# Block sums of an attention turned over by VectorE instead of TensorE, and layer 0's loads, flag and last nodes in another order

## The chip, the core and the metric

The kernel runs on one core of one Trainium2 chip, in one launch. The metric is device time in microseconds. A core has five engines that run side by side, each with its own queue of instructions in program order: TensorE (PE, matmul; its weight loads are listed as PEld), VectorE (DVE), ScalarE (ACT), GpSimd (POOL) and SyncE (SP, which here only issues DMAs). They meet through semaphores. SBUF is the working memory, PSUM the memory that matmuls write.

## The reference

There are N = 3327 nodes with D = 128 features and an adjacency matrix of 0 and 1. Layer 0 is a graph convolution, layer 1 an attention.

```python
# layer 0
h = max(layernorm(x), 0)
deg = adj.sum(1);  deg = where(deg == 0, 1, deg)
t = (adj.T @ h / deg) @ W_n.T + b_n + h @ W_c.T + b_c
x = x + relu(gamma * batchnorm(t) + beta)
# layer 1
h = max(layernorm(x), 0)
q, k, v = ((h @ W.T).reshape(128, 3327, 8) for W in (Wq, Wk, Wv))
a = softmax(q @ k.T / sqrt(128) + adj + adj, axis=2)     # 128 batches of 3327 x 3327
out = x + (a @ v).reshape(3327, 1024) @ Wo.T
```

The reshape doesn't split heads: it cuts the flat product into 128 batches of 3327 rows of 8 numbers.

## The kernel before

**Layer 0.** Nodes are cut into NC = 26 chunks of 128. For each chunk c a tile `a` of adj (128 x 3327) is loaded by SP (L431), PE adds `A[:, c, :].T @ a` into seven PSUM banks `acc` (L433), ScalarE sums the rows into `deg` (L437), VectorE takes their largest entry `amax` (L440), and one small piece of other work runs beside it (`beside`: turning the normalised nodes A into B, the product with W_c, the norms of Wq and Wk with GpSimd squares L406; `spread`: the reciprocals of deg laid along the columns, L410). x and the weights are loaded by DMAs issued from ScalarE's queue, x in two parts of 8 and 17 chunks, ahead of ScalarE's first work; all chunks are normalised (`stats`, `normalise`; L359 is VectorE's mean times reciprocal) before the loop over chunks.

Behind the loop, for each of the seven blocks of 512 columns: the mean (L506), the product with W_n (L507), the sum and its statistics (`hidden`); in between `spread` for the last two groups of chunks, and `set_flag` (L477), which computes from amax and the norms whether the softmax can go without a shift. Then batch norm and relu, residual, second layer norm, the columns of h in B, the projections of the first group of batches (`project_now`), the loads of its k, q and v, and writes to DRAM: `xd` (the nodes), `hd` (the columns of h), `wd` (exp(2 adj) for the last 8 chunks, a part of it; the rest is made during the first group).

**Attention.** The 128 batches are taken in NG = 32 groups of G = 4. The 3328 columns (queries) are cut into 7 blocks of QB = 476, the last 472. For each group and block, 26 chunks of 128 keys are gone through in SU = 13 steps, so there are 224 blocks and 2912 steps. A step takes four pairs (chunk, half); a half is two of the four batches. For each pair PE makes scores `s` for two batches side by side (`product`, L750), into one of three PSUM buffers of two banks each, which go round. Pairs are of two kinds:

- plain: VectorE adds adj to the scores (`add`, L862, which reads the tile `at` from SBUF and s from PSUM and writes a part of `d`); all plain pairs of a step then go through one exponential of ScalarE (L907), which is issued one step late.
- weighted: ScalarE takes the exponential f straight from s (L871) and GpSimd multiplies it by the loaded exp(2 adj), `wt` (L874).

Steps 3, 7 and 11 (`DOUBLE`) have two plain and two weighted pairs, all others three plain and one weighted. In a step the order is: the product and exponential of the first weighted pair; the exponential L907 of the step before; product and add of the first plain pair; half of the weighted sums of three steps earlier (`second(0)`, L623, PE); product and add of the second plain pair; the fourth pair; the other half of the sums (`second(1)`). In the step after a double one (4, 8, 12) the first product of the next step stands ahead of `second(1)`. Data for two steps later are requested by SP at a step's start (`fetch(x + PRE)`).

The sums of a block pile up in one of two PSUM tiles `av`: for batch b, rows 32b to 32b + 7 are the 8 sums and row 32b + 8 is the softmax denominator, all over the block's columns. They are finished by `finish`, a generator that goes on by one `yield` in each of the steps that `PARTS` names, in the block that follows (a block's last sums are issued in step 2 of the next one). Before: VectorE copies av into avs in step 3 (L633); PE turns it over by matmuls with a part of the identity in steps 5 and 6 (L640, two matmuls of the program in each, which the profile shows as four); in step 7, where `step()` stands between the first and the second add, VectorE takes the maximum of the denominators with 1e-30 (L648), the reciprocal (L649) and the product (L651); in step 8 SP stores the result to `att` (L658).

Later projections and the output product (`projections`, `outputs`: L208, L214, L234, L236, L269, L271, L279, L284) are slipped in at the end of steps 7 and 11, one part at a time, through the av tile that isn't in use. k of the next group is loaded into `ks` and sorted by GpSimd casts (L192).

The order on each engine is the program's: the kernel turns the framework's scheduler off (`manual_schedule`).

Of the kernel before, what the change touches and what calls it, by code (L numbers as in the profile page):

```python
# [20 lines left out]
H = 8  # L21
# [5 lines left out]
QB = 476  # L27
# [9 lines left out]
PARTS = (3, 5, 6, 7, 8)  # L37
# [9 lines left out]
def tile_two_layer_gnn(  # L47
# [42 lines left out]
    xd = dram.tile([NP, D], F32, name="xd")  # L90
# [13 lines left out]
    nc.gpsimd.memset(ov, 1.0)  # L104
    zeros = const.tile([P, H], F32, name="zeros")
# [98 lines left out]
    def projection(wk, hj, j, s, e, quick, ov, factor):  # L204
# [8 lines left out]
        if s == 2:  # L213
            nc.vector.tensor_copy(  # L214
                ov[:CH, e * 64 : (e + 1) * 64, :H],
                bank[:CH].rearrange("p (u h) -> p u h", h=H),
            )
            yield
            if e:
                nc.sync.dma_start(  # L220
                    v1[tok, :].rearrange("(p u) h -> p u h", u=D), ov[:CH]
                )
            return
        o = wk.tile([P, 2, NB], F32R, name="o")
        factor = 1.0 if s else factor
        if quick:
            nc.scalar.activation(o[:CH, 0], bank[:CH], AF.Copy, scale=factor)
            nc.vector.scalar_tensor_tensor(
                o[:CH, 1], bank[:CH], factor, o[:CH, 0].bitcast(F32), ALU.mult, ALU.subtract
            )  # L230
        else:
# [3 lines left out]
            else:  # L235
# [3 lines left out]
                o[:CH, 1], f[:CH], o[:CH, 0].bitcast(F32), ALU.subtract  # L239
            )  # L240
        yield
        for a in range(2):
            g = a * H + e * (H // 2)
            nc.sync.dma_start(
                (qT, kT)[s][g : g + H // 2, tok].rearrange("g (p u) -> p g u", u=D),
                o[:CH, a].bitcast(F32).rearrange("p (h u) -> p h u", u=D),
            )

    def projections(wk, hj, j, quick, ov, factor):
        return [  # L250
            projection(wk, hj, j, s, e, quick, ov, factor) for s in (1, 0, 2) for e in range(2)
        ]

    def outputs(wk, j):
# [7 lines left out]
        nc.sync.dma_start(xj[:CH], xd[j * CH : (j + 1) * CH, :])  # L262
# [38 lines left out]
    with tc.tile_pool(name="l0", bufs=1) as l0, tc.tile_pool(  # L301
        name="l0adj", bufs=3
    ) as ap, tc.tile_pool(name="l0s", bufs=2) as sp, tc.tile_pool(
# [18 lines left out]

        xr = x[: (NC - 1) * P, :].rearrange("(c p) d -> p c d", p=P)
        nc.vector.memset(xs[:, NC - 1, :], 0.0)
        for c0, c1 in ((0, 8), (8, NC - 1)):
            nc.scalar.dma_start(xs[:, c0:c1, :], xr[:, c0:c1, :])
        for p0, p1 in pieces(N - (NC - 1) * P):
            nc.scalar.dma_start(
                xs[p0:p1, NC - 1, :], x[(NC - 1) * P + p0 : (NC - 1) * P + p1, :]
            )  # L330
        nc.scalar.dma_start(wc, WcT)
        for i, b in enumerate((b_n, b_c, gamma, beta)):
            nc.scalar.dma_start(cols[:, i : i + 1], b.rearrange("o d -> d o"))
        nc.scalar.dma_start(wn, WnT)
        for t, w in zip(wqk, (WqT, WkT, WvT)):
            nc.scalar.dma_start(t, w)
        nc.scalar.dma_start(wo, WoT.rearrange("(e p) o -> p e o", p=P))
# [43 lines left out]
        stats(0)  # L381
        for i in range(NQ):
            if i + 1 < NQ:
                stats(i + 1)
            normalise(i, A)
        nc.vector.tensor_add(bias, cols[:, 0:1], cols[:, 1:2])

        def beside(x):
# [4 lines left out]
            elif x < 2 * NQ:  # L393
                n0 = (x - NQ) * NB
# [7 lines left out]
            elif x < 2 * NQ + 4:  # L402
                i = x - 2 * NQ
                sq = sp.tile([P, NB], F32, name="sq")
# [5 lines left out]
        def spread(i):  # L410
# [7 lines left out]
            dg = sp.tile([P, 4, P], F32, name="dg")  # L418
            for j in range(n):
                nc.gpsimd.tensor_scalar(  # L420
                    dg[:, j, :], ident, rdeg[:, 4 * i + j : 4 * i + j + 1], None, ALU.mult
                )
            nc.tensor.matmul(
# [4 lines left out]

        for c in range(NC):
            a = ap.tile([P, 7 * NB], F32, name="a")  # L430
            nc.sync.dma_start(a[:, :N], adj[c * P : (c + 1) * P, :])  # L431
            for i, (n0, w) in enumerate(blocks):
                nc.tensor.matmul(  # L433
                    acc[i][:, :w], A[:, c, :], a[:, n0 : n0 + w],
                    start=(c == 0), stop=(c == NC - 1),
                )
            nc.scalar.activation(  # L437
                junk, a[:, :N], AF.Copy, accum_out=deg[:, c : c + 1]
            )
            nc.vector.tensor_reduce(  # L440
                amax[:, c : c + 1], a[:, :N], AX.X, ALU.max, apply_absolute_value=True
            )
            if c >= 1:
                beside(c - 1)

            i = c - 2 * NQ - 5
            if 0 <= i < NQ - 2 and 4 * i + 4 <= c:
                spread(i)
        weights = []
        for n0 in range(0, NB, NB // 2):  # L450
            a = ap.tile([P, 7 * NB], F32, name="a")
            a8 = a[:, : 8 * (NB // 2)].rearrange("p (c n) -> p c n", c=8)
            nc.sync.dma_start(a8, adjr[:, WC:, n0 : n0 + NB // 2])
            weights.append((a8, n0, NB // 2))

        def weigh_early():
            a8, n0, w = weights.pop(0)
            nc.scalar.activation(a8, a8, AF.Exp, bias=low, scale=2.0)
            nc.sync.dma_start(wd[:, :, n0 : n0 + w].rearrange("c p n -> p c n"), a8)
# [5 lines left out]
        nc.vector.tensor_reduce(top, amax, AX.X, ALU.max)  # L465
        b = l0.tile([1, 6], F32, name="bound")
        for i in range(2):
            nc.vector.tensor_tensor(
                b[:, i : i + 1], norm[:, 2 * i : 2 * i + 1], norm[:, 2 * i + 1 : 2 * i + 2],
                ALU.max,  # L470
            )
        nc.vector.tensor_tensor(b[:, 0:1], b[:, 0:1], b[:, 1:2], ALU.mult)
        nc.vector.tensor_scalar(
            b[:, 0:1], b[:, 0:1], (1.001 * D * H * HALF) ** 2, None, ALU.mult
        )

        def set_flag():  # L477
# [9 lines left out]
            nc.vector.tensor_scalar(b[:, 5:6], b[:, 2:3], HALF, None, ALU.mult)  # L487
            nc.tensor.matmul(aside[:, :2], ones[:1, :P], b[:, 4:6], start=True, stop=True)
            nc.vector.tensor_copy(low_half, aside[:, :2])

# [13 lines left out]
        for i, (n0, w) in enumerate(blocks):  # L504
# [5 lines left out]
            if i in (0, 2):  # L510
                spread(NQ - 2 + i // 2)
            if i == 3:
                set_flag()
            if i in (4, 6):
                weigh_early()
# [16 lines left out]
        def keep_nodes(cs):  # L532
            nc.sync.dma_start(
                xd.rearrange("(c p) d -> p c d", p=P)[:, cs, :], xs[:, cs, :]
            )

        def residual(i):
            pt, cs = turned(i, A, acc[i])
            nc.vector.tensor_add(xs[:, cs, :], xs[:, cs, :], pt)
            if i < 3:  # L540
                keep_nodes(cs)

        def second_norm(i, engine):

            for c in range(4 * i, min(NC, 4 * i + 4)):
                engine.tensor_scalar(
                    C[:, c, :], xs[:, c, :], rs[:, c : c + 1], mr[:, c : c + 1],
                    ALU.mult, ALU.add,
                )
# [8 lines left out]
        def keep_columns(i0, i1):  # L558
            s = slice(4 * i0 * P, min(NC, 4 * i1) * P)
            nc.gpsimd.dma_start(hd[:, s], B2[:, s])  # L560

        def project_now(j, banks):
            todo = projections(sp, B2[:, j * CH : (j + 1) * CH], j, True, ov, low_half[:CH, 1:2])
            for p, b in zip(todo, banks):
                drive(p, b)
            for p in todo:
                drive(p)
                drive(p)
# [12 lines left out]
        stats(1, False)  # L581
        residual(2)
        project_now(0, [acc[j] for j in (6, 5, 4, 0)] + [aside, acc[1]])

        q, k, v = sets[0]
        ks = sets[1][1].rearrange("p c n -> p (c n)")
        for b in range(G):
            for args in k_loads(ks, 32 * b, b, 0, NP):
                nc.sync.dma_start(*args)
        for args in v_loads(v, 0):  # L590
            nc.sync.dma_start(*args)
        for i in range(4, NQ):
            relu(i)

        for b in range(G):
            for args in q_loads(q, 32 * b, b, 0, NB):
                nc.scalar.dma_start(*args)
        for i in range(2, NQ):
            if i > 2:
                residual(i)  # L600
            stats(i, False)
        nc.gpsimd.dma_start(
            xd.rearrange("(c p) d -> p c d", p=P)[:, 12:, :], xs[:, 12:, :]
        )
        roots(4, NC)
        factors(4, NC)
        for i in range(1, NQ):
            second_norm(i, nc.gpsimd if i % 3 == 0 else nc.vector)
        for i in range(1, NQ):
            columns(i, i % 2 == 0)  # L610
        for x, c in enumerate(range(0, NC, 4)):
            n = min(4, NC - c)
            (nc.scalar.copy if x % 2 else nc.gpsimd.tensor_copy)(
                k[:, c : c + n, :],
                ks.bitcast(F32).rearrange("g (p c) -> g c p", c=NC)[:, c : c + n, :],
            )
        keep_columns(0, NQ)
# [499 lines left out]
```

## Time and profile before

| | |
|---|---|
| time, median of 3 runs | 10375.15 us (10374.6 to 10377.76) |
| the profiled execution's own time | 10381.98 us |
| its span, first to last instruction | 10380.2 us |
| PE, ACT, DVE, POOL busy | 96%, 96%, 90%, 81% of the span |
| first step of the attention | about 264 us from the start |
| mean granted TensorE clock | 0.992 |

An engine's busy time is the time that its instructions cover; a matmul's end is modelled, so a busy PE is not PE at its peak. In the groups of instructions a row gives line, engine, operation, what is written and read, shapes and count, then busy time in us and the mean of one in ns, and then the idle time of the engine just before these instructions with what ended most of it. In a row of a window the columns are the window, its length, busy time (and instructions) of PE, PEld, DVE, ACT and POOL, then the granted clock, DMA share and GB/s. In a timeline row the columns are start, length (of several equal instructions together where a count stands behind), engine, line and operation; idle time ahead of it stands in brackets.

### The profile page before, as it was taken

How to read it: one execution, taken by the hardware profiler on the slowest of the kernel's cores; microseconds unless marked ns; L12 is line 12 of the kernel's file. 1: busy time of each engine (PE TensorE's matmuls, PEld its weight loads, DVE VectorE, ACT ScalarE, POOL GpSimd, SP SyncE). 2: the span in 40 equal slices, each digit the busy share in tenths (PEclk: the TensorE clock that was granted, in tenths of full speed). 3: DMA queues.
4: the chain of work that ended last, by engine and by line, in shares of the span. 5: the costliest groups of instructions: out<-in, count | busy, mean ns of one | idle time of the engine just before them, and what ended most of it. 6: DMA issues, size and time to landing. Idle time of an engine off the chain costs nothing. (4 is left out here: it accounts for less than half of the span.)

```text
span 10380.2 us, 189900 instructions
## 1 busy us (share of the span) xinstructions
PE 9995.3 (96%) x73327; PEld 3082.3 (30%) x73327; DVE 9366.9 (90%) x9533; ACT 9923.2 (96%) x6655; POOL 8439.0 (81%) x4317
## 2 busy tenths in 40 slices
PE   7899999999999999999999999999999999999999
PEld 3222222222222222222222222222222222222222
DVE  5789999999999999999999999999999999999998
ACT  4899999999999999999999999999999999999998
POOL 1678888888888888888888888888888888888887
PEclk9899999999999999999999999999999999999999
DMA  6766666666666666666665666666666665666554
GB/s 228 221 177 164 163 170 167 166 165 165 163 166 170 165 165 162 164 168 167 167 164 159 168 167 168 167 161 162 167 169 167 167 161 159 171 169 167 157 153 127
DMA packets 1114449, 1735.99 MB, mean 167 GB/s; under 512 B 194622, under 2 KB 1089980, under 8 KB 1105852
## 3 DMA queue, kind: packets, MB, share of 16 engines
q1 hardware_dynamic: 1108766, 1716.94, 60.9%
q8 instruction: 575, 9.42, 0.4%
q10 hardware_dynamic: 4350, 4.20, 0.1%
q14 instruction: 342, 2.80, 0.1%
q0 software_dynamic: 416, 2.63, 0.1%
HBM read 1621.05 MB, written 102.38 MB: 166 GB/s over the span
## 5 line engine op out<-in xcount | busy, mean ns | idle before, releaser
L862 DVE SCALAR_TENSOR_TENSOR d<-at,s 128x952 f32<-128x952 f32 x8064 | 8797.4, 1141 | 681.7 <-PE s L750 397.6
L874 POOL TENSOR_TENSOR f<-f,wt 128x952 f32<-128x952 f32 (+1 forms) x3584 | 7939.0, 2233 | 1674.3 <-ACT f L871 1649.9
L907 ACT ACTIVATE d<-d 128x2856 f32<-128x2856 f32 (+1 forms) x2912 | 7027.9, 2413 | 2.2 <-DVE d L862 1.9
L623 PE MATMUL av<-d,v 128*9 128x476 f32 x32256 | 5065.6, 566 | 0.7 <-ACT d L907 0.7
L750 PE MATMUL s<-q,k 32*128 32x476 f32 x23296 | 4087.3, 475 | 313.8 <-ACT f L871 243.5
L871 ACT ACTIVATE f<-s 128x952 f32<-128x952 f32 (+1 forms) x3584 | 3396.9, 970 | 281.8 <-PE s L750 266.0
L750 PEld LDWEIGHTS s<-q,k 32*128 32x128 f32 x23296 | 1739.5, 182 | 5500.2 <-DVE d L862 3005.9
L623 PE MATMUL av<-f,v 128*9 128x476 f32 x14336 | 2849.0, 566 | 0.0
L623 PEld LDWEIGHTS av<-d,v 128*9 128x9 f32 x32256 | 583.3, 88 | 1161.5 <-issue 1149.6
L640 PE MATMUL av<-ident,avs 128*119 128x36 f32 (+1 forms) x1792 | 474.1, 391 | 0.8 <-DVE avs L633 0.8
L640 PEld LDWEIGHTS av<-ident,avs 128*119 128x119 f32 (+1 forms) x1792 | 422.9, 308 | 103.1 <-issue 101.5
L623 PEld LDWEIGHTS av<-f,v 128*9 128x9 f32 x14336 | 316.6, 88 | 112.4 <-issue 88.7
L192 POOL CAST k<-ks 128x256 fp32r<-128x256 f32 x434 | 283.8, 654 | 0.0
L433 PE MATMUL acc<-a,A 128*128 128x512 f32 (+1 forms) x364 | 151.6, 569 | 24.2 <-ACT A L367 23.4
L238 POOL TENSOR_TENSOR o<-pf,o 104x512 fp32r<-104x512 f32 x124 | 160.0, 1291 | 9.9
L633 DVE COPY avs<-av 128x476 f32<-128x476 f32 (+1 forms) x224 | 145.4, 649 | 4.6 <-PE av L623 4.6
L440 DVE TENSOR_REDUCE amax<-a 128x1 f32<-128x3327 f32 x26 | 93.7, 3611 | 36.4 <-DMA a<-in_adj 36.4
L433 PEld LDWEIGHTS acc<-a,A 128*128 128x128 f32 x364 | 69.0, 192 | 109.0 <-issue 84.5
L236 DVE TENSOR_SCALAR pf<-av,low_half 104x512 f32<-104x512 f32 x62 | 46.6, 751 | 46.8 <-PE av L208 46.6
L406 POOL TENSOR_TENSOR sq<-wk 128x512 f32<-128x512 f32 x2 | 2.1, 1042 | 102.5 <-PE aside L407 102.5
L234 DVE COPY pf<-av 104x512 f32<-104x512 f32 x62 | 42.9, 692 | 46.9 <-PE av L208 46.9
L437 ACT ACTIVATE junk<-a 128x3327 bf16<-128x3327 f32 x26 | 77.5, 2979 | 7.1 <-DMA a<-in_adj 6.8
(123 smaller groups left out, 1032.3 us busy)
## 6 DMA issues: line engine op xcount, KB each, us to landing
at<-in_adjT SPq DMA_DIRECT2D x1728, 476.0 KB
wt<-wd SPq DMA_DIRECT2D x1536, 238.0 KB
at<-in_adjT SPq DMA_DIRECT2D x288, 472.0 KB
wt<-wd SPq DMA_DIRECT2D x256, 236.0 KB
ks<-kT SPq DMA_DIRECT2D x496, 104.0 KB
q<-qT SPq DMA_DIRECT2D x496, 104.0 KB
a<-in_adj SPq DMA_DIRECT2D x26, 1663.5 KB
kT<-o SPq DMA_DIRECT2D x128, 208.0 KB
```

The source lines that it names most:

```text
L192: nc.gpsimd.tensor_copy(k[:, c : c + n, half * 64 : half * 64 + 64], ks.bitcast(F32).rearrange("g (p c) -> g c p", c=NC)[:, c : c + n, :],)
L238: nc.gpsimd.tensor_tensor(o[:CH, 1], f[:CH], o[:CH, 0].bitcast(F32), ALU.subtract)
L433: nc.tensor.matmul(acc[i][:, :w], A[:, c, :], a[:, n0 : n0 + w], start=(c == 0), stop=(c == NC - 1),)
L440: nc.vector.tensor_reduce(amax[:, c : c + 1], a[:, :N], AX.X, ALU.max, apply_absolute_value=True)
L623: nc.tensor.matmul(av[32 * b : 32 * b + H + 1, :w], tiles[2][:, b, c, :], e, start=first, stop=last,)
L633: nc.vector.tensor_copy(avs[:, : R * J], av[:, : R * J])
L640: nc.tensor.matmul(pt[:R, j, :], avs[:, j : j + (R - 1) * J + 1 : J], some, start=True, stop=True)
L750: nc.tensor.matmul(p[:, x, :we], k[rs, c, :], q[rs, n0 : n0 + we], start=True, stop=True,)
L862: nc.vector.scalar_tensor_tensor(d[:, j, :, :w], have[0, i, y, c // 2][:, c % 2, :w] .unsqueeze(1).to_broadcast([P, 2, w]), SAFE / 2, p[:, ...
L871: nc.scalar.activation(f[:, :, :w], p[:, :, :w], AF.Exp, scale=2.0)
L874: nc.gpsimd.tensor_tensor(f[:, :, :w], f[:, :, :w], have[1, i, y, c][:, :w].unsqueeze(1).to_broadcast([P, 2, w]), ALU.mult,)
L907: nc.scalar.activation(flat, flat, AF.Exp, scale=2.0)
```

## The change

**The block sums.** QB is 480, so that the blocks have 6 x 480 and 448 columns, all multiples of 32. `finish` has three parts instead of five, in steps 3, 7 and 8. The copy becomes a VectorE transpose in patches of 32 x 32 straight from PSUM: for each j, the 32 columns q·J + j of batch b go to partitions 32b + q. The maximum reads avs (in SBUF) and a constant tile `tiny`, the product reads avs and ri. Four stores (one for each batch) take the place of one; the last block needs eight.

```diff
-QB = 476
+QB = 480
-PARTS = (3, 5, 6, 7, 8)
+PARTS = (3, 7, 8)
+    tiny = const.tile([P, 1], F32, name="tiny")
+    nc.vector.memset(tiny, 1e-30)
...
     def finish(rp, av, d0, n0, w):
-        J = 4
-        R = -(-w // J)
-        avs = rp.tile([P, QB], F32, name="avs")
-        nc.vector.tensor_copy(avs[:, : R * J], av[:, : R * J])
+        J = -(-w // 32)
+        avs = rp.tile([P, QB // 32, 32], F32, name="avs")
+        nc.vector.transpose(
+            avs[:, :J, :].rearrange("p j h -> p (j h)"),
+            av[:, : 32 * J].rearrange("p (q j) -> p j q", j=J),
+        )
         yield
-        pt = av[:, : J * G * (H + 1)].rearrange("p (j q) -> p j q", j=J)
-        some = ident.rearrange("p (b h) -> p b h", h=32)[:, :, : H + 1]
-        for j in range(J):
-            nc.tensor.matmul(
-                pt[:R, j, :], avs[:, j : j + (R - 1) * J + 1 : J], some, start=True, stop=True
-            )
-            if j % 2:
-                yield
-        pv = pt.rearrange("p j (b h) -> p b j h", h=H + 1)
-        ri = rp.tile([P, G, J], F32, name="ri")
-        nc.vector.tensor_scalar(ri[:R], pv[:R, :, :, H], 1e-30, None, ALU.max)
-        nc.vector.reciprocal(ri[:R], ri[:R])
-        o = rp.tile([P, G, J, H], F32, name="oq")
+        ri = rp.tile([P, QB // 32], F32, name="ri")
         nc.vector.tensor_tensor(
-            o[:R], pv[:R, :, :, :H], ri[:R].unsqueeze(3).to_broadcast([R, G, J, H]),
+            ri[:, :J], avs[:, :J, H], tiny.to_broadcast([P, J]), ALU.max
+        )
+        nc.vector.reciprocal(ri[:, :J], ri[:, :J])
+        o = rp.tile([P, QB // 32, H], F32, name="oq")
+        nc.vector.tensor_tensor(
+            o[:, :J, :], avs[:, :J, :H], ri[:, :J].unsqueeze(2).to_broadcast([P, J, H]),
             ALU.mult,
         )
         yield
-        nc.sync.dma_start(attb[...], o[:r]...)
+        for b in range(G):
+            ab = att[...].rearrange("(q j) h -> q (j h)", j=J)
+            ob = o[32 * b : 32 * b + 32, :J, :].rearrange("q j h -> q (j h)")
+            nc.sync.dma_start(ab[:r], ob[:r])
...
```

**Layer 0.** All large loads stand in SP's queue: the first four chunks of x, then adj, with the rest of x and the large weights between the chunks of adj; the small weights are issued by GpSimd, none by ScalarE. Each group of four chunks is normalised within the loop instead of ahead of it. A tile of four pieces (`small`) serves the squares, the diagonal of `spread` and the first projections. The bound's first part is computed within the loop; `set_flag` and the last `spread` stand in the last chunk, in the middle of its matmuls.

```diff
+        nc.sync.dma_start(xs[:, :4, :], xr[:, :4, :])
+        def load(c):
+            a = ap.tile([P, 7 * NB], F32, name="a")
+            nc.sync.dma_start(a[:, :N], adj[c * P : (c + 1) * P, :])
+            ...
+        load(0)
+        for c in range(NC):
+            a = tiles[c]
+            if c + 1 < NC:
+                load(c + 1)
+            if c < NQ:
+                if c == 0:
+                    stats(c)
+                normalise(c, A)
+                if c + 1 < NQ:
+                    stats(c + 1)
...
+            last = c == NC - 1
+            gather(0, 4 if last else len(blocks))
...
+            if last:
+                nc.vector.tensor_reduce(top, amax, AX.X, ALU.max)
+                flags = set_flag()
+                next(flags)
+                gather(4, len(blocks))
+                next(flags)
+                spreading = spread(NQ - 1)
+                next(spreading)
```

Behind the loop, the first group's projections are taken apart, k first, its stores on SP and those of q and v on GpSimd, with relu, residual and statistics of the other blocks between them; the second norm is shared by ScalarE, VectorE and GpSimd. `xd` is stored as [128, 26, 128] by one DMA of GpSimd at the end of layer 0, where before three were SP's and one GpSimd's; `hd` is stored in two parts. The loads of k, q and v of the first group move into the attention, to SP, behind the loads of the first two steps (`fetch(PRE - 1)`, `first_loads`), and the sort of k is shared by three engines. The pools of the attention stand in another order, with that of `d` first.

```diff
+                def first_loads():
+                    ...
+                    for b in range(G):
+                        for args in k_loads(ks, 32 * b, b, 0, NP):
+                            nc.sync.dma_start(*args)
+                    for b in range(G):
+                        for args in q_loads(q, 32 * b, b, 0, NB):
+                            nc.sync.dma_start(*args)
+                    ...
+                fetch(PRE - 1)
+                first_loads()
```

More of the change, by code (lines that the diff above doesn't have):

```diff
@@ L261, in outputs @@
         xj = wk.tile([P, D], F32, name="xj")
-        nc.sync.dma_start(xj[:CH], xd[j * CH : (j + 1) * CH, :])
+        for c in range(j * CH // P, ((j + 1) * CH - 1) // P + 1):
+            m0, m1 = max(j * CH, c * P), min((j + 1) * CH, (c + 1) * P)
+            nc.sync.dma_start(
+                xj[m0 - j * CH : m1 - j * CH], xd[m0 - c * P : m1 - c * P, c, :]
+            )
         tT = wk.tile([P, H, P], F32, name="t4")
@@ L422, in spread @@
                 )
+            yield
             nc.tensor.matmul(
@@ L449, in tile_two_layer_gnn @@
[L449 to L459, printed above, removed]
@@ L464, in tile_two_layer_gnn @@
-        top = l0.tile([P, 1], F32, name="top")
[L465 to L475, printed above, removed]
+            yield
@@ new lines, in tile_two_layer_gnn, with set_bound @@
+        top = l0.tile([P, 1], F32, name="top")
+        b = l0.tile([1, 6], F32, name="bound")
+        def set_bound():
+            for i in range(2):
+                nc.vector.tensor_tensor(
+                    b[:, i : i + 1], norm[:, 2 * i : 2 * i + 1],
+                    norm[:, 2 * i + 1 : 2 * i + 2], ALU.max,
+                )
+            nc.vector.tensor_tensor(b[:, 0:1], b[:, 0:1], b[:, 1:2], ALU.mult)
+            nc.vector.tensor_scalar(
+                b[:, 0:1], b[:, 0:1], (1.001 * D * H * HALF) ** 2, None, ALU.mult
+            )
@@ L509, in tile_two_layer_gnn @@
                 hidden(i - 1)
[L510 to L514, printed above, removed]
+            if i == 0:
+                next(spreading)
+            if i in (0, 1):
                 weigh_early()
```

252 lines of the change are left out of this document (139 added, 113 removed).

## The prediction

> **What bounds the kernel now.** I read the page first, then the busy time by window, ScalarE's groups after the first group of batches, and last one block of columns instruction by instruction.
>
> ```profile
> PE 9995.3 (96%) x73327; PEld 3082.3 (30%) x73327; DVE 9366.9 (90%) x9533; ACT 9923.2 (96%) x6655; POOL 8439.0 (81%) x4317
> L907 ACT ACTIVATE d<-d 128x2856 f32<-128x2856 f32 (+1 forms) x2912 | 7027.9, 2413 | 2.2 <-DVE d L862 1.9
> L871 ACT ACTIVATE f<-s 128x952 f32<-128x952 f32 (+1 forms) x3584 | 3396.9, 970 | 281.8 <-PE s L750 266.0
> ```
> ```profile
> 5000.00:6000.00 1000.00, 973.17 (x7266) 298.07 (x7266) 918.43 (x927) 975.03 (x649) 838.26 (x426) 1.00 0.61 164
> ```
> ```profile
> L871 ACT ACTIVATE f<-s 128x952 f32<-128x952 f32 (+1 forms) x3468 | 3287.0, 971 | 234.8 <-PE s L750 220.4 <-POOL k L192 14.4
> ```
>
> ScalarE does the two exponentials and hardly stops: 97.5% of a steady window, at full granted clock (1.00). PE's 97% is less telling, since its matmuls overlap: it still finds room for more than a microsecond of transposes twice in a block. From 651 us on, ScalarE's listed idle time is 234.8 us before f (L871). There are 31 groups of 7 blocks after that point, so 217 blocks: 1.08 us a block. One block shows where; f7 below is the first f of step 7.
>
> ```profile
> 5139.32 2.61 ACT L907 ACTIVATE d<-d 128x2856 f32<-128x2856 f32 x1
> 5142.55 0.97 ACT L871 ACTIVATE f<-s 128x952 f32<-128x952 f32 x1 [0.62 <-PE s L750]
> 5146.47 0.97 ACT L871 ACTIVATE f<-s 128x952 f32<-128x952 f32 x1 [0.48 <-POOL k L192]
> 5153.18 0.97 ACT L871 ACTIVATE f<-s 128x952 f32<-128x952 f32 x1
> 5154.02 2.61 ACT L907 ACTIVATE d<-d 128x2856 f32<-128x2856 f32 x1
> ```
> ```profile
> 5140.06 1.06 PE L640 MATMUL av<-ident,avs 128*119 128x36 f32 x4
> 5143.98 1.06 PE L640 MATMUL av<-ident,avs 128*119 128x36 f32 x4
> 5149.85 0.49 PE L750 MATMUL s<-q,k 32*128 32x476 f32 x4
> 5150.27 0.99 PE L623 MATMUL av<-d,v 128*9 128x476 f32 x8
> 5151.19 1.18 PE L750 MATMUL s<-q,k 32*128 32x476 f32 x6
> ```
>
> Both of the block's stops, 0.62 and 0.48 us, come behind a pair of L640 transposes (steps 5 and 6): 1.06 us stand in PE's queue ahead of the weighted sums, and those ahead of the product for the next f. In this block a GpSimd cast ended close to the second product and is named as the releaser; over all blocks 220.4 of the 234.8 us are put down to PE.
>
> **Sums and their transposes.** Removed: 8 matmuls a block on PE, 1792 in all. Steps 5 and 6 then look like steps 9 and 10, which have the same work without L640 and next to no stop, so I take the whole 1.08 us a block. 223 blocks end inside the loop: 223 x 1.08 = 241 us gone.
>
> VectorE's copy from PSUM (0.65 us) becomes a transpose of 128x480 at the same place, after the last add of step 3. No row shows a transpose; the nearest is that copy, same source, same size. Step 3 has two adds instead of three, and the next add but one must wait for a ScalarE release anyway (0.5 us of VectorE gap there), so a transpose of up to 1.2 us is free and I add nothing. [...]
>
> Width 480 for 476: 6 x 480 + 448 = 6 x 476 + 472 = 3328, the same columns and the same number of instructions: nothing. One att store becomes four, of 32 x 480 B; before it moved 476 pieces of 128 B. A store's issue takes about 0.32 us of SP; three more are 1 us in a 44.7 us block on a queue that mostly waits, and they stand where the one stood (step 8). Behind them are the loads for two steps later: nothing.
>
> **The three small operations.** They keep their place, between the two adds of step 7. What changes is their operands. Before, the maximum read PSUM and a constant, and the product read PSUM and ri. Now the maximum reads avs and tiny, the product avs and ri: both inputs in SBUF. VectorE's steady loop has had no such instruction so far (its add reads at from SBUF and s from PSUM). Layer 0 has one beside GpSimd work:
>
> ```profile
> 26.72 0.92 DVE L359 SCALAR_TENSOR_TENSOR ln_mr<-ln_mv,ln_rs 128x4 f32<-128x4 f32 x1
> 28.80 0.16 DVE L359 SCALAR_TENSOR_TENSOR ln_mr<-ln_mv,ln_rs 128x4 f32<-128x4 f32 x1
> 26.59 2.04 POOL L406 TENSOR_TENSOR sq<-wq 128x512 f32<-128x512 f32 x2 [23.20 <-DMA wq<-in_WqT]
> ```
>
> Four columns took 0.92 us instead of 0.16. They ended at 27.64, with the first of GpSimd's two 1.04 us operations (26.59 to 27.63). The statistics and reciprocals beside the second one, with one SBUF input, kept their durations. So I read: with two SBUF inputs VectorE stands until the running GpSimd operation is over.
>
> [...]
>
> What GpSimd and VectorE do in step 7 now:
>
> ```profile
> 5146.51 1.15 DVE L862 SCALAR_TENSOR_TENSOR d<-at,s 128x952 f32<-128x952 f32 x1 [0.49 <-ACT d L907]
> 5147.57 0.17 DVE L648 TENSOR_SCALAR ri<-av 119x16 f32<-119x16 f32 x1
> 5147.77 0.25 DVE L649 RECIPROCAL ri<-ri 119x16 f32<-119x16 f32 x1
> 5148.06 0.29 DVE L651 TENSOR_TENSOR oq<-av,ri 119x128 f32<-119x128 f32 x1
> 5148.27 1.14 DVE L862 SCALAR_TENSOR_TENSOR d<-at,s 128x952 f32<-128x952 f32 x1
> 5147.51 2.23 POOL L874 TENSOR_TENSOR f<-f,wt 128x952 f32<-128x952 f32 x1 [1.06 <-ACT f L871]
> ```
>
> GpSimd starts its product 1.04 us after f7 starts and holds until 3.27; all times from here count from the start of f7. Without the two stops ScalarE is earlier against VectorE, so the first add of step 7 starts not at 0.04 but at about 0.4 (as in steps 3 and 11), and the maximum is due at 1.4, in the middle of GpSimd's product. By the layer 0 row it ends with it, at 3.29. Reciprocal and product follow as in the rows (0.03 + 0.25 + 0.04, then 0.21 to the next add): the second add starts at 3.82 and ends at 4.96.
>
> Is that on the path? Three PSUM buffers go round. The first product of step 8 needs the buffer that this add empties: matmul at 5.02, add at 5.54. PE then has 0.42 + 0.92 us (5149.85, 5150.27, 5151.19) before the other two products of step 8: 6.36, and with 0.49 for the product and a handoff the second add is at 6.88. The third starts 1.06 later (the spacing 5146.51 to 5147.57), at 7.94, and ends at 9.08; d of step 8 can start at 9.17. ScalarE, if it never waits, is there at 5154.02 - 5146.47 = 7.55. So it stands 1.62 us a block: 223 x 1.62 = 361 us. Turned round, the second add must start by 2.20 to cost nothing; without the wait it would start at about 2.1.
>
> Bounds of that cost. If the maximum slips in before GpSimd and only the product waits, the add starts at 3.21: 1.0 us. If a cast (0.68 us) pushes GpSimd's product back in some blocks: up to 2.0. None at all is the rival. I take 1.62, since GpSimd's start and its 2.23 us are rows, and 1.4 lies 0.4 after 1.04.
>
> **Layer 0.** The first matmul starts at 23.45: x landed at 13.57, then ScalarE still had DMA issues until 20.86. Now the first four chunks of x (256 KB) go ahead of adj on SP, and ScalarE issues none: 12 us earlier, between 0 and 15, for from there PE is busy chunk after chunk (6.0 to 6.4 us each). Flag and last row sums move into the last chunk: two VectorE stops of 3.5 and 2.7 us (198.29, 204.75) and their small operations go, 8 us, between 0 and 10. The first add of the attention waited until 271.80 for the write of hd, and ScalarE 8.9 us with it; the add's buffers now lie elsewhere: 8 us, between 0 and 9. Against it, 16 q loads leave ScalarE's queue, where they took 12 us, for SP, behind two adjacency loads and the eight k loads, and the first product stays behind k: 0, between a gain of 5 and a loss of 8. 12 + 8 + 8 = 28 us of gain, from 15 to 40.
>
> **Sum.** The profiled execution took 10381.98 (span 10380.2), 6.8 more than the median 10375.15. 10382 - 241 + 361 - 28 = 10474, less 7: 10467.
>
> **Rivals.** *No wait between VectorE and GpSimd that counts* (the side of faster). For it: only one instruction shows the wait, of another kind, in another stage. Against it: its end agrees with GpSimd's to 0.02 us. It decides where the second add of step 7 starts: by 2.20, all is free. Then 10382 - 241 - 28 - 7 = 10106.
>
> *The wait is there, but shorter* (only the product waits): 223 x (1.0 - 1.08) = -18, so 10382 - 18 - 28 - 7 = 10329.
>
> *A dear transpose.* At four times the copy, 2.6 us, it passes its cover by 1.4: 223 x 1.4 = 312 more than either case. Nothing in the trace speaks for it.
>
> **How the numbers follow.** Full wait 0.60, its own range 10390 to 10520 (1.3 to 1.85 us a block, layer 0 15 to 40); no wait 0.30; short wait 0.06; dear transpose 0.04. What a measurement of this kernel can tell from no change is about 0.2%, 21 us. Faster: no wait (0.30) and most of the short one (0.04): 0.34. Same: the low edge of the full wait (0.05) and 0.01 of the short one: 0.06. Slower: the rest, 0.60. The range must reach both signs: 10085 (no wait, layer 0 at its best) to 10520.
>
> **What would show it.** In the changed profile: L640 gone and no stop before f of steps 5 and 6; the maximum lasting some 1.9 us and ending with GpSimd's product; ScalarE idle about 1.6 us before f and d of step 8, released by PE and VectorE; the transpose near 0.65 us; the first matmul near 11 us. Wrong if the maximum takes 0.2 us, or takes 1.9 and ScalarE does not stop.

## The result, and the profile after

| | before | changed |
|---|---|---|
| time, median | 10376.45 us (4 runs) | 10671.85 us (4 runs) |
| ratio, 95% interval | | 1.0284 [1.0266, 1.0302] |
| profiled execution: its own time, span | 10381.98, 10380.2 | 10676.35, 10674.5 |
| mean granted TensorE clock | 0.992 | 0.961 |

The change costs 295 us; the forecast was 92 above the median it was made against (10467 for 10375). The time lies outside the forecast range of 10085 to 10520.

The page of the changed kernel, with the busy shares, and the groups of ScalarE's two exponentials, the maximum and the transpose:

```profile
PE 10007.4 (94%) x71535; PEld 2762.0 (26%) x71535; DVE 9697.3 (91%) x9528; ACT 9941.2 (93%) x6662; POOL 8440.0 (79%) x4329
L969 ACT ACTIVATE d<-d 128x2880 f32<-128x2880 f32 (+1 forms) x2912 | 7040.3, 2418 | 177.0 <-DVE d L924 175.3
L933 ACT ACTIVATE f<-s 128x960 f32<-128x960 f32 (+1 forms) x3584 | 3417.0, 980 | 409.2 <-PE s L784 385.3
L684 DVE TENSOR_TENSOR ri<-avs,tiny 128x15 f32<-128x15 f32 (+1 forms) x224 | 428.9, 1915 | 0.0
L677 DVE STREAM_TRANSPOSE avs<-av 128x480 f32<-128x480 f32 (+1 forms) x224 | 150.4, 671 | 4.4 <-PE av L667 4.4
```

ScalarE's idle time ahead of d rose from 2.2 to 177.0 us and ahead of f from 281.8 to 409.2, though the transposes on PE (L640) are gone. The maximum of 15 columns takes 1.92 us on average. The 1000 us in the middle, as the prediction showed them of before (window, length, busy time of PE, PEld, DVE, ACT, POOL, granted clock, DMA share, GB/s):

```profile
5000.00:6000.00 1000.00, 947.21 (x6872) 258.48 (x6868) 923.01 (x898) 946.46 (x628) 812.60 (x413) 0.96 0.58 160
```

ScalarE is busy 94.6% where it was 97.5%, and the granted clock is 0.96 where it was 1.00. The clock is the line that the prediction had no term for. One block shows both. First VectorE, GpSimd and ScalarE around step 7 (f7 starts at 5256.44):

```profile
5256.44 1.01 ACT L933 ACTIVATE f<-s 128x960 f32<-128x960 f32 x1
5257.83 1.98 DVE L684 TENSOR_TENSOR ri<-avs,tiny 128x15 f32<-128x15 f32 x1
5259.84 0.25 DVE L687 RECIPROCAL ri<-ri 128x15 f32<-128x15 f32 x1
5260.13 0.28 DVE L689 TENSOR_TENSOR oq<-avs,ri 128x120 f32<-128x120 f32 x1
5260.33 1.15 DVE L924 SCALAR_TENSOR_TENSOR d<-at,s 128x960 f32<-128x960 f32 x1
5257.52 2.25 POOL L936 TENSOR_TENSOR f<-f,wt 128x960 f32<-128x960 f32 x1
5263.99 0.97 ACT L933 ACTIVATE f<-s 128x960 f32<-128x960 f32 x1 [0.62 <-PE s L784]
5265.71 2.61 ACT L969 ACTIVATE d<-d 128x2880 f32<-128x2880 f32 x1 [0.74 <-DVE d L924]
5269.45 0.97 ACT L933 ACTIVATE f<-s 128x960 f32<-128x960 f32 x1 [1.13 <-PE s L784]
```

GpSimd's product starts 1.08 us after f7, the maximum 1.39, and they end 0.04 us apart; the second add starts at 3.89 (forecast 3.82) and d of step 8 at 9.27 (forecast 9.17). The third stop, 1.13 us before f of step 10, was not forecast. PE's queue in the same block, and the busy times in four slices of 3.41 us:

```profile
5259.87 0.48 PE L784 MATMUL s<-q,k 32*128 32x480 f32 x2
5261.53 0.48 PE L784 MATMUL s<-q,k 32*128 32x480 f32 x2 [1.18 <-DVE d L924]
5264.59 1.01 PE L667 MATMUL av<-d,v 128*9 128x480 f32 x2
5265.54 0.77 PE L784 MATMUL s<-q,k 32*128 32x480 f32 x2
5266.23 1.36 PE L667 MATMUL av<-d,v 128*9 128x480 f32 x8
5268.35 0.57 PE L667 MATMUL av<-d,v 128*9 128x480 f32 x2
```
```profile
5256.78:5260.20 3.42, 3.42 (x24) 0.93 (x16) 3.35 (x5) 3.42 (x3) 3.00 (x3) 1.00 0.41 124
5260.20:5263.61 3.41, 2.23 (x18) 0.68 (x16) 3.25 (x5) 3.18 (x3) 2.74 (x2) 1.00 0.15 25
5263.61:5267.02 3.41, 3.41 (x20) 0.54 (x18) 2.60 (x3) 2.28 (x2) 3.41 (x2) 0.50 0.98 274
5267.02:5270.44 3.42, 3.42 (x32) 0.80 (x24) 2.94 (x4) 2.29 (x3) 0.48 (x1) 1.00 0.73 186
```

PE stands 1.18 us for the late add. In the slice that holds the gap it is busy 2.23 of 3.41 us, and in the next slice the clock is granted at half: a pair of weighted sums takes 1.01 us there and 0.57 in the slice after it, a product of scores 0.77 instead of 0.48. From 700 us on the trace has 126 such stretches, nearly all of 3.41 us or a multiple of it, 709 us together; in the profile of before it has 2, both at the very end of the run (15.9 us).

### The profile page after: what moved, and what is told of

It is laid out like the page before. It is cut to its first block, busy times and chain, and to the rows that moved or that the text cites. A ratio compares the mean times of both kernels' runs of the same rounds, so it can differ in the third digit from the quotient of the medians.

```text
span 10674.5 us, 187296 instructions
## 1 busy us (share of the span) xinstructions
PE 10007.4 (94%) x71535; PEld 2762.0 (26%) x71535; DVE 9697.3 (91%) x9528; ACT 9941.2 (93%) x6662; POOL 8440.0 (79%) x4329
## 5 line engine op out<-in xcount | busy, mean ns | idle before, releaser
L936 POOL TENSOR_TENSOR f<-f,wt 128x960 f32<-128x960 f32 (+1 forms) x3584 | 7937.0, 2230 | 2000.3 <-ACT f L933 1968.7
L924 DVE SCALAR_TENSOR_TENSOR d<-at,s 128x960 f32<-128x960 f32 x8064 | 8739.2, 1140 | 716.3 <-PE s L784 588.3
L969 ACT ACTIVATE d<-d 128x2880 f32<-128x2880 f32 (+1 forms) x2912 | 7040.3, 2418 | 177.0 <-DVE d L924 175.3
L667 PE MATMUL av<-d,v 128*9 128x480 f32 x32256 | 5279.6, 587 | 0.6 <-ACT d L969 0.6
L784 PE MATMUL s<-q,k 32*128 32x480 f32 x23296 | 4334.7, 488 | 614.0 <-DVE d L924 367.3
L933 ACT ACTIVATE f<-s 128x960 f32<-128x960 f32 (+1 forms) x3584 | 3417.0, 980 | 409.2 <-PE s L784 385.3
L784 PEld LDWEIGHTS s<-q,k 32*128 32x128 f32 x23296 | 1840.7, 186 | 6102.7 <-DVE d L924 4077.9
L667 PE MATMUL av<-f,v 128*9 128x480 f32 x14336 | 2967.1, 583 | 0.0
L684 DVE TENSOR_TENSOR ri<-avs,tiny 128x15 f32<-128x15 f32 (+1 forms) x224 | 428.9, 1915 | 0.0
L677 DVE STREAM_TRANSPOSE avs<-av 128x480 f32<-128x480 f32 (+1 forms) x224 | 150.4, 671 | 4.4 <-PE av L667 4.4
```

The source lines that it names most:

```text
L667: nc.tensor.matmul(av[32 * b : 32 * b + H + 1, :w], tiles[2][:, b, c, :], e, start=first, stop=last,)
L677: nc.vector.transpose(avs[:, :J, :].rearrange("p j h -> p (j h)"), av[:, : 32 * J].rearrange("p (q j) -> p j q", j=J),)
L684: nc.vector.tensor_tensor(ri[:, :J], avs[:, :J, H], tiny.to_broadcast([P, J]), ALU.max)
L784: nc.tensor.matmul(p[:, x, :we], k[rs, c, :], q[rs, n0 : n0 + we], start=True, stop=True,)
L924: nc.vector.scalar_tensor_tensor(d[:, j, :, :w], have[0, i, y, c // 2][:, c % 2, :w] .unsqueeze(1).to_broadcast([P, 2, w]), SAFE / 2, p[:, ...
L933: nc.scalar.activation(f[:, :, :w], p[:, :, :w], AF.Exp, scale=2.0)
```

## The experiments

The theory was: VectorE's two-SBUF-input operations wait for GpSimd; the second add of step 7 comes late and ScalarE stops (the loss that was forecast); and the gap that this leaves on PE brings the half clock, which adds the rest. The rivals: something else that the change brought is dear (transpose, stores, the new layer 0), or the clock is a by-product without a price.

**One input from PSUM.** The floor and the reciprocals go to spare columns of the block's sums in PSUM.

```diff
-        ri = rp.tile([P, QB // 32], F32, name="ri")
+        least, ri = av[:, QB : QB + 1], av[:, QB + 1 : QB + 1 + QB // 32]
+        nc.vector.memset(least, 1e-30)
         nc.vector.tensor_tensor(
-            ri[:, :J], avs[:, :J, H], tiny.to_broadcast([P, J]), ALU.max
+            ri[:, :J], avs[:, :J, H], least.to_broadcast([P, J]), ALU.max
         )
```

> As the changed kernel, but the floor 1e-30 and the reciprocals stand in spare columns 480 to 495 of the block's sums in PSUM, so that the maximum and the product read one input from SBUF and one from PSUM. Theory (the two SBUF inputs make VectorE's maximum wait for GpSimd's running product; the second add of step 7 comes late, ScalarE and then TensorE stand, and the granted clock halves in about half of the blocks): the maximum falls from 1.96 us to about 0.2, ScalarE's idle time before d of steps 7 and 8 goes back to a few tenths of a us, the mean granted clock is near 0.99 and the time near 10376 - 241 (before L640's stops) - 27 (layer 0) = 10108, between 10085 and 10150. Rival A (the dear part is something else that the change brought: the transpose out of PSUM, the four stores per block or the wider block): the time stays above 10500 although the maximum is short. Rival B (the delay costs what was predicted, 361 us, and the clock falls for a reason of its own): near 10300 with the clock still near 0.96.

Measured: 10074.29 us (4 runs), ratio to before 0.971 [0.9695, 0.9725], clock 0.994. The maximum and ScalarE's groups in this kernel, and in the block of the same number the maximum and GpSimd's product:

```profile
L684 DVE TENSOR_TENSOR av<-avs,av 128x15 f32<-128x15 f32 (+1 forms) x224 | 42.2, 189 | 7.7
L969 ACT ACTIVATE d<-d 128x2880 f32<-128x2880 f32 (+1 forms) x2912 | 7064.4, 2426 | 7.3 <-DVE d L924 2.8
L933 ACT ACTIVATE f<-s 128x960 f32<-128x960 f32 (+1 forms) x3584 | 3443.5, 988 | 35.4 <-PE s L784 24.1
```
```profile
4978.10 0.19 DVE L684 TENSOR_TENSOR av<-avs,av 128x15 f32<-128x15 f32 x1
4977.60 2.25 POOL L936 TENSOR_TENSOR f<-f,wt 128x960 f32<-128x960 f32 x1
```

The maximum takes 0.19 us at the same place, 0.5 us into GpSimd's product. ScalarE is busy 999.54 of the 1000 us from 5000. So two SBUF inputs cost the changed kernel 598 us, and nothing else in the change is dear: rival A falls, and rival B with it, since the clock came back at once. The time lies 11 us below the expected 10085 to 10150: the finish and layer 0 together gained 302 us where 268 were reckoned.

**The same operations, earlier.** Two SBUF inputs stay; the three small operations go ahead of the first add of step 7, where GpSimd's product of step 6 ends and that of step 7 has not begun.

```diff
+                    if s == DOUBLE[1]:
+                        step()
                     add(0, product(i, y, *plain[0]))
                     second(0)
...
-                    if s == DOUBLE[1]:
-                        step()
                     add(1, product(i, y, *plain[1]))
```

> As the changed kernel, two SBUF inputs and all, but maximum, reciprocal and product are issued ahead of the first add of step 7, so before GpSimd's running product of step 7 begins. Theory: the maximum takes about 0.2 us where GpSimd is idle, the trio 0.7 us in all, and the time falls to that of the kernel with one SBUF input or up to 100 us above it (10100 to 10210), since the first add of step 7 now stands behind 0.7 us; granted clock near 0.99. Rival (the three small operations are dear wherever they stand, or the delay is that of the trio's own length in front of an add): over 10450.

Measured: 10068.66 us, ratio 0.9702 [0.9688, 0.9717], clock 0.993. In the profile of this kernel the same instruction as in the changed one:

```profile
L684 DVE TENSOR_TENSOR ri<-avs,tiny 128x15 f32<-128x15 f32 x192 | 33.9, 176 | 0.0
```

Two SBUF inputs alone cost nothing here (0.18 us); in the changed kernel, beside GpSimd's running product, the same instruction took 1.92. In 30 blocks of this kernel a GpSimd cast runs beside the product L689, and the product takes 0.41 us for 0.28. The expectation, 10100 to 10210, was too high: no price of the earlier place shows, and the time agrees with that of the kernel with one SBUF input within their spread. These two are the fastest of the runs, 3% below the kernel before.

**The gap on PE filled.** The wait stays; PE gets matmuls with zero weights where it stands (they add zero to the sums).

```diff
+    nothing = const.tile([P, H + 1], F32, name="nothing")
+    nc.vector.memset(nothing, 0.0)
...
+                    if s == 8 and due:
+                        (fi, fy, _), fe = waiting[0]
+                        for x2 in range(4 if begun else 8):
+                            b = x2 % 4
+                            nc.tensor.matmul(
+                                avs2[(fi * len(qblocks) + fy) % 2][32 * b : 32 * b + H + 1, :w],
+                                nothing, fe[0][:, b % 2, :w], start=False, stop=False,
+                            )
                     add(0, product(i, y, *plain[0]))
```

> As the changed kernel, wait and all, with 4 to 8 further weighted-sum matmuls per block whose weights are zeros, placed on TensorE ahead of the sums that stand in the gap of step 8, so that TensorE has work while ScalarE waits; the output is unchanged by them. Theory (the gap on TensorE lets the granted clock fall, and that is the part of the 295 us that the prediction left out): VectorE's maximum stays near 1.96 us, the granted clock goes from 0.961 to 0.99 and the time from 10672 to about 10480 to 10510, which is the forecast of record and a little for the added matmuls. Rival A (the clock is a by-product and costs nothing on the path): the clock rises, the time stays within 30 us of 10672. Rival B (the clock does not depend on TensorE's gap): neither moves, or the added matmuls make it slower.

Measured: 10416.10 us, ratio 1.004 [1.0025, 1.0056], clock 0.994. Lines of its profile: the maximum, the gap on PE in the block of the same number, and the middle window.

```profile
L686 DVE TENSOR_TENSOR ri<-avs,tiny 128x15 f32<-128x15 f32 (+1 forms) x224 | 426.9, 1906 | 0.0
```
```profile
5145.54 0.99 PE L955 MATMUL av<-d,nothing 128*9 128x480 f32 x8
5146.76 0.48 PE L786 MATMUL s<-q,k 32*128 32x480 f32 x2 [0.23 <-DVE d L926]
```
```profile
5000.00:6000.00 1000.00, 969.33 (x7294) 267.07 (x7286) 945.16 (x923) 970.40 (x647) 834.97 (x426) 1.00 0.60 164
```

The maximum waits as long as in the changed kernel, PE's gap is 0.23 us instead of 1.18, the clock is full, and 256 us are gone (10671.85 - 10416.10). The added matmuls do not bend this: blocks without a half-clock stretch take 45.35 us in the changed kernel, and all blocks here take 45.36 (the first six of groups 3 to 31; 43.79 in the kernel with one SBUF input). The loss from the delay alone is 1.57 us a block, 342 us in the times (10416.10 - 10074.29). Rival A, the free clock, falls, and rival B, a clock that does not depend on PE's gap.

The expected 10480 to 10510 was too high: of the 64 us to its lower end, 32 are the base (the kernel without the wait took 10074, not the forecast's 10106), 19 the wait (342 for 361), and 13 were meant for the added matmuls, which cost nothing that shows.

**Layer 0 alone.** The new order of layer 0 with the finish of before (its copy, four transposing matmuls and one store, QB 476, five PARTS).

```diff
-QB = 480
+QB = 476
-PARTS = (3, 7, 8)
+PARTS = (3, 5, 6, 7, 8)
-        nc.vector.transpose(...)
+        nc.vector.tensor_copy(avs[:, : R * J], av[:, : R * J])
...
```

> Only the other order in layer 0 (loads, flag, last nodes), with the block finish of before: copy, four transposing matmuls, one store, blocks of 476. Theory: 12 us from the first matmul and 15 from the node sums and the flag stay, and the steady state is that of before: 10376 - 27 = 10349, between 10340 and 10360, granted clock 0.99. Rival (a part of the 295 us sits in the new order, as later loads or another start of the queues): at or above 10376.

Measured: 10357.19 us (11 runs), ratio 0.9981 [0.9972, 0.999]: 19 us less than before, between 10 and 29, and within the expected 10340 to 10360. In the profiled runs the first step of the attention starts 22 us earlier (241.5 for 264.0) and the first group ends 28 us earlier (622.7 for 651.2). Against this kernel the one with one SBUF input shows what the finish is worth without the wait: 10357.19 - 10074.29 = 283 us.

**A delay without two SBUF inputs.** On the kernel with one SBUF input, two maxima on VectorE that nobody reads, ahead of the finish's own; then only one of them.

```diff
+    busy = const.tile([P, 2], F32, name="busy")
...
+        nc.vector.tensor_reduce(busy[:, 0:1], wqk[0][:, :770], AX.X, ALU.max)
+        nc.vector.tensor_reduce(busy[:, 1:2], wqk[1][:, :770], AX.X, ALU.max)
         least, ri = av[:, QB : QB + 1], av[:, QB + 1 : QB + 1 + QB // 32]
...
```

> As the kernel with floor and reciprocals in PSUM (no operation of the finish has two SBUF inputs; it took 10074 us), with two maxima of 770 columns each on VectorE ahead of the finish's own maximum: extra work of about 2 x 0.85 us, with one SBUF input and a result that nothing reads. Theory (what is dear is the lateness of the second add of step 7, whatever makes it late, and the idle TensorE behind it): the add starts near 3.9 us after the start of f of step 7 as in the changed kernel, ScalarE idles about 1.6 us per block, windows of half clock come back, and the time is 10600 to 10700 with a granted clock near 0.96. Rival (GpSimd's use of SBUF beside VectorE's two inputs is itself needed for the loss): the extra work hides and the time stays below 10250.

> The same with one of the two added maxima, about 0.85 us. Theory of delay alone: the second add of step 7 starts near 3.1 us where 2.2 would be in time, 0.7 to 0.9 us per block, so 10074 + 224 x 0.8 = 10250. Theory of the clock on top: in the changed kernel the clock fell after each 3.41 us window of a fixed grid in which TensorE stood for more than 1.1 to 1.3 us together, and never after one with less than 1.08; before, the fullest such window had 0.95. A delay of 0.85 takes some windows past that bound: half clock in some blocks, less often than in the changed kernel, and 10280 to 10400 with a clock between 0.965 and 0.99. If the clock fell with any gap, it would fall as often as in the changed kernel: 10450 or more.

Measured: 10523.21 us with both (10505.87 to 10543.04; ratio 1.0146 [1.0129, 1.0163], clock 0.976) and 10405.92 us with one (7 runs; ratio 1.0028 [1.0017, 1.004], clock 0.977). Each added maximum took 0.94 us. Blocks at full clock throughout take 45.40 and 44.68 us, 1.61 and 0.89 more than the 43.79 without a delay. So the lateness of the add is what costs, whatever makes it late, and 1.61 is close to the 1.57 of the wait; the rival (below 10250) falls. Half clock comes back with the delay alone: 373 us of it after 700 us in each. The full dose missed its expectation (10600 to 10700) by the clock, which fell less often than in the changed kernel; the direct part was as expected. The half dose came out a little above its 10280 to 10400: 0.89 us a block for 0.8 expected, and a clock of 0.977 within the expected 0.965 to 0.99.

**Only the product waits.** The floor in PSUM, the reciprocals in SBUF: the maximum has one SBUF input, the product two.

```diff
+        least = av[:, QB : QB + 1]
+        nc.vector.memset(least, 1e-30)
         nc.vector.tensor_tensor(
-            ri[:, :J], avs[:, :J, H], tiny.to_broadcast([P, J]), ALU.max
+            ri[:, :J], avs[:, :J, H], least.to_broadcast([P, J]), ALU.max
         )
```

> As the changed kernel, but the maximum has its floor in PSUM and so one SBUF input; the product keeps its two. Theory: the maximum takes 0.2 us, the product waits for the end of GpSimd's running product (near 3.3 us after the start of f of step 7) and ends near 3.6, so the second add starts 0.3 to 0.4 us sooner than in the changed kernel: a direct loss of 1.2 us per block, 10074 + 265 = 10340, and windows of half clock in some blocks on top, 10400 to 10560. Rival (the product does not wait, only the maximum did): near 10075.

Measured: 10468.03 us, ratio 1.0088 [1.0071, 1.0105], clock 0.974. The two operations in this kernel, groups and then one block with GpSimd's product:

```profile
L690 DVE TENSOR_TENSOR oq<-avs,ri 128x120 f32<-128x120 f32 (+1 forms) x224 | 302.7, 1352 | 7.9 <-DVE ri L688 0.2
L685 DVE TENSOR_TENSOR ri<-avs,av 128x15 f32<-128x15 f32 (+1 forms) x224 | 40.4, 181 | 7.7
```
```profile
5152.74 0.18 DVE L685 TENSOR_TENSOR ri<-avs,av 128x15 f32<-128x15 f32 x1
5153.24 1.39 DVE L690 TENSOR_TENSOR oq<-avs,ri 128x120 f32<-128x120 f32 x1
5152.25 2.24 POOL L937 TENSOR_TENSOR f<-f,wt 128x960 f32<-128x960 f32 x1
```

The wait has moved to the product: it ends at 5154.63, 0.14 us after GpSimd's product (5154.49), and takes 1.35 us on average. Blocks at full clock take 44.86 us, 1.07 over those without a wait (1.2 expected); the rest is clock (445 us at half after 700 us). The time lies within the expected 10400 to 10560.

**The transpose twice.** On the kernel with one SBUF input, L677 is issued a second time.

> As the kernel with floor and reciprocals in PSUM, with the 32x32 transposes of a block done twice: 0.67 us more on VectorE per block. Theory (the transpose has up to 1.2 us of cover where it stands): 0.67 + 0.67 = 1.34 us is about 0.1 to 0.2 past the cover, so 10074 to 10120 and a granted clock of 0.99. Rival (VectorE, busy 93% of the span, has no slack there, and the price of the transpose is part of the 295 us): 10074 + 224 x 0.67 = 10225.

Measured: 10130.28 us, ratio 0.976 [0.9744, 0.9776], clock 0.992. The second transpose takes 0.68 us and costs 56 us, 0.25 a block. Blocks at full clock take 43.99 us, 0.20 more than the 43.79 with one transpose; the rest is a few half-clock stretches, 8 of 3.41 us before the end of the run. If a microsecond past the cover costs a microsecond, some 0.48 us of cover are left behind the first transpose, and the whole cover is about 1.15 us: the prediction said "up to 1.2". So the single transpose costs nothing there, and the rival (10225) falls. The slip of 10 us past the expected 10120 is about what the half-clock stretches add.

## Why the prediction was wrong

The sign and the wait were right; the size was not. The runs split the 295 us into the prediction's terms. Each measured term is the difference of two neighbours in a chain of kernels from before to changed, so the sum closes by itself and confirms nothing:

| term | forecast, us | measured, us | from |
|---|---|---|---|
| finish without L640 | -241 | -283 | one SBUF input against layer 0 alone |
| layer 0 | -28 | -19 (-29 to -10) | layer 0 alone against before |
| wait between VectorE and GpSimd | +361 | +342 | gap filled against one SBUF input |
| granted clock | no term | +256 | changed kernel against gap filled |
| sum | +92 | +296 | changed kernel against before |

**The step that failed** is the end of the sum: the loss was taken to stop at d of step 8, with no term for the granted clock, as if PE kept full clock whatever it waited for. Up to that point the reckoning held. Medians over the first six blocks of groups 3 to 31 (the last such block left out), in us after f7:

| | d of step 8 | f of step 10 |
|---|---|---|
| forecast | 9.17 | no loss behind d of step 8 |
| gap filled | 9.26 | 11.78 |
| changed, 87 blocks without a half-clock stretch | 9.26 | 11.77 |
| changed, 86 blocks with one | 9.36 | 13.05 |

Blocks with a half-clock stretch take 47.26 us, those without 45.35. This is the third stop of the block shown: half clock from 5263.61 to 5267.02, PE's products and sums 0.77 and 1.36 us long where they take 0.48 and 0.99, and 1.13 us of idle time before f at 5269.45. Over the kernel it is the 256 us that no term stood for.

The prediction read "full granted clock (1.00)" in the window of before as a fact of the steady state. The runs show it as a state that goes when PE stands longer (0.96 in the same window of the changed kernel, 1.00 there with PE's gap filled). The working that put the matmul behind the second add at 5.02 also says that PE stands until then; this was priced as a delay of ScalarE and not looked at as idle time of PE. The range failed with it: the "full wait" case ended at 10520 because its spread was that of the delay alone. Its ends don't come out of the stated pieces exactly either (no wait with layer 0 at 40 is 10094, not 10085; 1.85 us a block with layer 0 at 15 is 10531, not 10520), but neither reaches 10672.

**The wait.** One layer-0 row of four columns (0.92 us for 0.16) was enough to read it rightly: maximum 1.98 us, end beside GpSimd's, second add at 3.89 for 3.82, d of step 8 at 9.27 for 9.17, and 1.57 us a block for 1.62. The runs show it for this maximum and product: the maximum takes 1.92 us beside GpSimd's product with two SBUF inputs, 0.19 with one, and 0.18 with two ahead of GpSimd's product; where only the product has two, it takes 1.35 beside GpSimd's, and 0.28 behind it in the block of the changed kernel.

**L640's 1.08 us** was too small. ScalarE's steps 5 and 6 took 4.07 and 3.91 us before (medians) and take 3.35 each with one SBUF input: 1.28 us less, against listed idle time of 0.61 + 0.48. The other 0.2 us fits the overlap that the rows show: an exponential that doesn't wait starts some 0.1 us before the one ahead of it ends, and one that follows a stop has no such overlap. In the kernel with one SBUF input:

```profile
4984.20 2.61 ACT L969 ACTIVATE d<-d 128x2880 f32<-128x2880 f32 x1
4986.71 0.95 ACT L933 ACTIVATE f<-s 128x960 f32<-128x960 f32 x1
```

f starts at 4986.71 and d ends at 4986.81. Here the idle time of a stop is thus a lower bound of what its removal brings; the difference of the starts is the whole.

**Free as forecast:** the transpose (0.67 us; forecast about 0.65), the width of 480 and the four stores: with the wait away, ScalarE has no stop left to put down to them. **Layer 0** came near: the first matmul starts at 8.47 us (forecast 11, before 23.45), and the attention's first step 22 us earlier; the interval of the gain holds the 28.

**The rivals.** "No wait" was priced near (10106; 10074 once the wait is taken away), but the wait came. "Only the product waits", priced at 10329, takes 10468 when built so: 1.07 us a block for 1.0 and again the clock.

## What to carry to other kernels

Before an operation of VectorE is given a second input from SBUF, see what GpSimd runs at that place: here the maximum took 1.92 us beside GpSimd's product, and 0.19 with a constant in a spare PSUM column or 0.18 a microsecond earlier. When a delay leaves TensorE standing, price its clock as well (256 us here): look at how much PE already stands in the fullest stretches of 3.41 us (0.95 us in the kernel before) and how much the delay adds, first of all where PE has no other work to put into the gap (with the half delay 61 of 62 such blocks were hit, and 0 of 139 others). The idle time listed before an instruction can be less than what its removal brings: here neighbouring exponentials overlap by 0.1 us, and 1.09 us were listed for a gain of 1.28.

## What the runs showed of the hardware

In the changed kernel the granted clock falls on a fixed grid: all 126 half-clock stretches from 700 us on start within 0.01 us of one phase of a 3.4133 us raster; they last 3.41 or 6.83 us as a rule. Cut on that raster, from 700 us to 40 us before the end, each window at full clock has a time in which PE stood (no matmul record covers it; a missing record would add to it):

| kernel | fullest stand in a window that was followed by full clock | least in one followed by half | windows followed by half |
|---|---|---|---|
| before | 0.95 us | none | 0 |
| gap filled | 0.98 | none | 0 |
| half delay | 1.04 | 1.10 | 66 |
| only the product waits | 1.19 | 1.08 | 77 |
| changed | 1.28 | 1.08 | 124 |
| full delay, one SBUF input | 1.70 | 1.14 | 89 |

The kernel before lived with up to 0.95 us, 0.13 under the least of the table that half clock followed. What the delay made of it went with PE's other work. As a rule a part of the projections or of the output product stands at the end of step 7 in five of a group's seven blocks, ahead of the gap; in two there is none. The median of PE's longest stand there, and the blocks of groups 3 to 31 with a half-clock stretch behind it (the last block of the run left out):

| kernel | with such a part: stand, blocks hit | without: stand, blocks hit |
|---|---|---|
| half delay | 0.83 us, 0 of 139 | 1.53 us, 61 of 62 |
| only the product waits | 0.67, 12 of 139 | 1.70, 59 of 62 |
| changed | 1.16, 52 of 139 | 2.19, 62 of 62 |
| full delay, one SBUF input | 1.69, 23 of 139 | 1.53, 58 of 62 |

The half delay shows it best: the same 0.94 us on VectorE brought half clock in nearly every block where PE had nothing else to do, and in none where it had. But neither the length of one stand nor its sum over a window decides alone. With the full delay PE stands longer in the blocks with such a part and is hit less there, and 78 windows with 1.2 us or more kept the clock; with the transpose done twice all 8 falls came after only 0.73 to 0.97. What else the clock goes by was not found out.

In the changed kernel the clock fell after windows in which PE stood for between 1.08 and 2.21 of the 3.41 us, and the longest single stand that reached into one of them was 2.22 us.
